# A written-out instruction order for a graph network, replaced by another from the same search

## The chip, the cores and the metric

The kernel runs on one core of one Trainium2 chip. The time is device microseconds of one execution; the kernel before took 2856.57 us as the median of three runs (2853.59 to 2860.73). One execution was also recorded by the hardware profiler: that is the profile below. The line numbers (L1916) are those of the kernel before; every line of the kernel after ORDER stands three lines lower once the change is made.

## The reference

A batch of 32 node sets x (512 nodes, 256 features each) passes through four layers over one 512 x 512 adjacency matrix. After each layer the layer's input is added to its output and the sum is normalised over its features.

```python
# layer 0: 8 heads of 32; scores = q k^T / sqrt(32), masked by adj, softmax, times v; norm;
#          relu(x w1 + b1) w2 + b2; norm
# layer 1: one additive head; e = leaky_relu(s1[i] + s2[j]), masked, softmax, times h
# layer 2: e = leaky_relu((x W1)(x W2)^T), masked, softmax, times (x W3), relu
# layer 3: 4 additive heads of 64, masked, softmax, times q, elu
x = _layernorm(x + _L0_gnn_ref(x, adj, ...), axis=-1)
x = _layernorm(x + _L1_gnn_ref(x, L1_gnn_W, L1_gnn_a, adj), axis=-1)
x = _layernorm(x + _L2_gnn_ref(x, adj, L2_gnn_W1, L2_gnn_W2, L2_gnn_W3), axis=-1)
x = _layernorm(x + _L3_gnn_ref(x, adj, L3_gnn_W, L3_gnn_a), axis=-1)
```

All of it is float32.

## The kernel before, in words

Each of the 32 node sets is a graph of about 340 steps. A step is one call of `plan(engine, ns, run, reads, writes, ...)`: an engine, a planned duration, the function that issues its instructions, and the buffers that it reads and writes. All graphs have the same steps, and some seven of them are under way at any time. `prepare` (L1624) adds the steps that load and rearrange weights and masks.

**What sets the order.** For each of the five engines (PE, DVE, ACT, POOL, SP), ORDER holds one long string. A letter names the graph (`.` is `prepare`, `A` is graph 0, `f` is graph 31), and digits ahead of a letter say how many of that graph's waiting steps on this engine are skipped. So the strings are the queues of the engines, written out. They came from a search that was done beforehand and is not in the file. Within an engine the queue is in order: a step that waits holds up every step behind it.

`Plan.follow` (L1411) reads the strings and then replays the queues with the planned durations. From that replay come three things only: which of its kind's buffers a step gets (the one that comes free first in the replay), the order in which the instructions are emitted, and nothing that delays an instruction on the chip. `Plan.ways` (L1395) picks for each projection or product whether it runs as whole 128 x 128 matmuls or as four 128 x 32 column tiles, so that PE changes its array mode less often.

PE works in three modes, and each change between neighbouring steps costs time: whole array (transposes L1784, L1867, L1899, L2059 and most of L1595), row tiles (`exps`, L1916: the scores of four heads at once, 32 rows each) and column tiles (the heads' products L1974 and L2180, the sums L1947 and L2156, and the rest of L1595).

**The steps that the text speaks of.** In layer 0, `exps` makes scores in four PSUM banks, ACT exponentiates them into a `p` buffer (L1920, four instructions), DVE multiplies the whole buffer by the mask (L1967), and PE multiplies by v (L1974). The sums over heads are made by adding `p` buffers to one another with accumulating DMAs that POOL issues (`add_dma`, L1854), and one more DMA from SP; a `p` buffer is free only when these have landed. There are eight `p` buffers. The last graph makes its sums on PE instead (`at_once`).

In layers 1 and 3, `gates` (L2044) transposes a few scores on PE (L2059), sends them to DRAM and back spread over all partitions (two DMAs from SP), and DVE builds the attention from them (L2086, L2165), masks it (L2089, L2172), and PE uses it (L1595, L2180). `add` (L1842) is an addition or product on POOL; `normalise` is L1825 and L1826 on DVE, L1829 and L1830 on ACT, L1832 on DVE, L1835 on ACT.

`load` in `prepare` (L1625) issues one weight or mask DMA from SP. In the plan each is a step of 450 ns. Graph inputs x are loaded from SP as well (L2218, 512 KB each), results stored (L2224). After the last step a short check of ranges runs on DVE and PE (L2243 to L2251).

```python
for e, steps in order.items():
    queues[e], at = [], 0
    for step in steps:
        if step.isdigit():
            at = 10 * at + int(step)
        else:
            queues[e].append(left[e, GRAPHS.index(step) - 1].pop(at))
            at = 0
```

The file holds `Plan`, `fast_path` and what is in it twice; the later copy (from L1325) is the one that runs.

Of the kernel before, what the change touches and what calls it, by code (L numbers as in the profile page):

```python
# [32 lines left out]
        "AA2.2...A2A1.2A.AA.1...A2.A1..1A1BB2AA2AA1BABAA1B1AB2ABA2ABABA1BCA2BC3BC4BB3C2C4BBBCCBCB1B2BBCDABABA"  # L33
        "D1CACDDDAADAA1CAAD2C3CDCCB2CEBCABBA2AA1AA2CEA3CCCBBCBBDB1AAAAECB1D1AEAD1AA1A1AAABAAB1DBDB1A1AAACBDCB"
        "CDCEB1AEAE1A2A1AAD1CCDAC1BBB1DB2DCDEC2DDDBBCBBDB1B1B1BBBAEFB2B1BB1CC1ACCACDCA1EDBBDDCE1E1B1BB2EFBFFB"
        "3EEAEEDC1CACAA1EDCDD2EFE2EDDCCEE2C1CECCCCCCB1FFC1CCC1DDFFE1B1D1DDBECDB1FEEDCGG1CCC2FFFC1G1FFGB1FBDD"
        "1EEC1BBF1F1DDEE2F3FEFGFCF1DDE3DDDDDDDDGFGD2DDDGEEG1E1ECFECDFEFFC1GDHEHD2D2G1HD3GDGCGHGFD2E1GGCECCEF"
        "1G1FFEG1GFF2GGDEEGEGEH2E2E3E2E1EEHH1EEE1FFE1F1FFHDGDHGFGGED1HEF1II3EEE2HEIH2HHIDH1HGFDEF1DDGFG2HFGH"
        "2HHGH1HFGIFEHHFFFFFFFFIIF1FFFGGI2G2GGGEHEHIHFHE1IF1JJGF1FF2IJIFI1IIEHJEGFIIEHGGE1IGHIH1II1IJ1HHGGFII"
        "2GGGGGGGGJJG1GGG1HHJHIHHFFJIHGIIF1JG1KKH1GG2J3JGGJJKFJIKGFH1JJFHFH1JIH2JIIJJ1JIIGJJ1HHKHH1H1HHHHH1KK"  # L40
        "1HH1HHIIGK1IIIGJKJIJHJG1KH1LLIH1H2KKHL2KHKKGJHLJGI1KGK1I1KGIJIJ2K3KJKJKHIIKK1IILI1I1I1I1ILIL1I1IIIJJ"
        "L2JJJHKHLKJ1KKIH1LIJMM2III2LMILL1LML1LIHJLHKKHHJ1LJ2LJ1KK3LLKLIKL1JJMLJJ1J1J1J1J1JJ1MM1J1JJJMKKI2K1K"
        "LKIMLK1LJLJI1M1NKN1JJ2MMN1JJ2MLMINM1MJKIMIKILK1MLLK2M3MM1LMLJM1KKNMKK1K1K2K1K1K1NKNK2K1KKLLNJLJM1LNM"
        "1LLMMJ1KK1N1OKL1KOK2NNOO2NJKNNJMKL1NNJLM1NJ1MLML2NNO2NMMLLNKNNLLL1L2L1LLL1OO2L1LLLMMO1MK1MNKON1MM1NN"
        "LK1OL1PMPL2LL2OPOO1OKLONKPNLK1OMK1N2O2MMMN1OO1ONO1ONLO1MMP3M1MMMMMMOM1PPM2MMM1NNLN1NPNLOPONOOML1PM1Q"
        "QNMM2P1MMQ3PLPQP2PLOMN1LLPNP1PONONO2PPO2PPMONNQ1NNPPN1N1NNNNQQNNNNOOQOOOMMPQPOPNNPM1QR3NONR2Q1NQQN1Q"
        "RNR2QMOQQMO1PMMO1QPOP2QP3QRQPQNQPOOQOOO1O1O1O1OORRO2OOOR1PPN2PPPQNQRQPOQN1ROPSS1O1O2RRORSO1RNQSNQOR"
        "1RPRNPN1R2RPPQQRR1RSQPQPRROPPP1P1PPPPSS1PP1PP1QSQR1OQ1QQOSRQRRPO1STPQT2PP2S1PSPS1SO1TTROPSQSSOQO1SRQ"
        "1RQR2SSR2STSQRQSPS1QQQ1Q1Q1Q1QQTT1Q1QQQ1RRTRTPS1RRPSRSSQQP1TU1QRQU2T1QQUT2TTTPSQU1TPR2TTS1PRR1SPSR2T"
        "ST2TRSQTTTRURRR1RRRRRUU1R2R1RRSSQ1SUSTQSUTSTRRQ1UT2RS2URVV1RR3UUVUQUVTRSQUUQQ1S1UTS1TTS2UUU1U1TTRUSS"  # L50
        "VSSUS3S1S1S1SS1VV1SSSVTSTVRUTRTU1TTU1SUSWR1VWTS2VS1SSV2VWRVUWRST1R2VVV1VRU1TUUTT2V3VWVUUVS1TTVVTT1T"
        "1TTTTTWW2TTTTUUW2UUUSVSVW1VVUTS1WT1XXU3T1TT2WWWT1WVXTWSX1WUW1WSU1SSVUUVV2WVVU3WWTWWUX1UUUUUUUUXWX1U"
        "1U1UUVXV1T1V1VWTWVXWVU1XTUWVYY1U2XX2UXUU1XYYWUTXTV1XXTT1VVW1XVWW2XXW2XWXUXX1VVYVV1VVVVVVYYVVV1WWVY1W"
        "2WWXWUXYUV1XXU1YVZZVW2VV2YVYY1YZU1XVZXUY1YWYU1WU1YW1X2YYXWXYX1YV1WZWYWYWW1W1W1W1WWZZ2W2W1WW1XXZ1XZXY"
        "VVYXX1YY1WWV1Za1WXWaW2Za3ZZWZ2ZVZYaXVWX1VYVZXX1ZYY2ZZZ1Z1YYWZ1XaXZ2X1XXXXXXXaa2XX1XYXYa1YYYWWZaZYZXZ"
        "W1aXY1bb1X1XX2aXabZ2aWaaWbXY1aaWZW1Y1aYY1ZZ2a3aZZabXaaYYa1YYY1Y1Y1Y1YYbbY1YYYZZbZZXZaXbYaZ1aaX1bZYcc"
        "YY2bcb1YYb1bXbacXYZZ1XaX1bZ2bZ1aa3b1bab2babYbZZc1ZZZ1Zb1ZZZZ1cc1ZZZZaacaaYbYcbaabbYZdZa1cd3Z1ZZ2cZcc"
        "d1cYc1cbdZacYaYY1cbabab2c3c1bccbZaac1acdaa1a1a1aaadda1aaad1bbZbZc1bdbcb1cacaZ1de1abeaa2ddad1deZd1dZa"
        "ebcc1bZZbb2ddc2d3dcedcca1bbddbdbbbbbbbee1b1bbb1cecda2cedadcccbda1ebfcf1bb2ee1bb2eefea1efbca1d1adcacc"
        "2ee1dd2e3eede1fe1ccdfc2ccc1cecccbfc1ccc1ddffbdd1fdefbed1ceceb3fd1ff2ff3c2c1cc4ff1ffbf1f2f3ffedcbe3fb"  # L60
        "e1ddff2f2ffffbffdeeedddd1ffdffdffdddcdeeff3f1f1ffdfdddc3e2eeece1fffcddf1d2d1deedeedcfcf1cceeeeeeeeee"
        "1ff1eeee1ff1fffefedeeeefefff1ddffd2fffffe1ed1edeffffd1ffedeee1fffff"
    ),
    "DVE": (
        ".1...6..5.3.8.1.9.7..1.4.4.1.1.3.3.5.5.1.4.1.1.2.4.4.4.4.1.3.3.3.1.2.2.2.2.2.AA.A1.A....AAAABB1BBBBB"
        "BA2ACAAAAAAACA1A1AAAAACA1A1AA2AAAACABCB1B2BBB1BBCBC3AA1AAAC1AB4AA2B2AA1A1BAAADB1BBBBBB1BBBBBDBAAAAAA"
        "AAD1A1AAA1A1A1A1AC2C1ACAC1C1C1CCCDBB1BBBD1B1B3BB1BBBBDDB2AC1C1A1CAA1A1ADCCCACA2ACC2CC1CCBCBBCBBBBBAC"
        "2A1A1AAA3BB1BBA1B1B1B1BA1AAA1BEBD2DDD1DDEDEDC1CCECDCC1CAEC3CAA2CC5B1CCBAECEBBB2ADE2D1DADB5BA1DD1ABD"
        "1BA2BDCCCDCC3DCCCDDD1DDBA2BD1BC1BB1BC1BC2CCB3C2CB1CB1CEFEE1E3EF1E1E1EF2DE2D1DDDCFDBDB3D2DBF1DDFDCDC"
        "1CCDCFFEB2E1E2BE1EBEBEBCBEEEEE2D2DDDDDDD1C1E1EEE1CCBCD2D2CD1CCDC1D2D4C1D1DDC2CD1CCCFF1FFF2FFGFGFGEEE"  # L70
        "EEGCCE1E2ECGE1EG2DDDE1EEDEDFG2FGC1F2CFFFCDFD2CD1CFFC10DFEEEF1EEEEFE2FFFDFD1EDDCE1DED1DE1E1E1E1EDDD1E"
        "DGE1G4GG1GHG1GGHH1FGFFFFHFD1D3FDFF1FH1FFH1EEFEEFEGHDH2D1DDGG1GDGGDEGGGG1GGFEFFFEFDFFF2G1GGE2EGEEFE2E"
        "F2E1FFEFEF2FEFFEEFH2HH2H1HH1HIHIHI1GGGGGIEEG3GG2GGIE1GIG1FGFFFGIFIHH3H1H1HHEHFF1F1EE2HHHHE1EGEGGHGGE"
        "GGG3F2H1HHFH1FGF1G3FGG2G1G4F2GFF1F1GFFGGFIII1I2I2IJIIJIJ1H1HHHHJH3HFFFHHJ1H1HJHG1GH1GGGJHJIFF2I1G2F"
        "2FGGII1II1FFI7GIIIHH1IHIHHHHH2I1IIGFIG1GG1HH1H1GH2H1H3GGG2H1H1GG1HGJ2J1JJK1J1J1JJKJHKI2IIIIKGGKI1HIG"
        "I3I1I1II1HI1HHKIHKKHG1GJ1JJ1G1JHGJ1GJGJ8HJ1HII1JIIIJIII8H1JJJJJ3HJHG2H1IHI1H1IIIIHI1IH1HIHIHKK1KKKL"
        "2KKKLKL1J2J1JJJLHHJ3JHJ2JLLJJJJ1II1IIJILLKH1K2H1K1HKHK1HKHK1IKKI2KHJIJJKJJJJ1KKJ1KK4I6IKII2I5I1JII1J"
        "JJ1JII1JJ1JJIJILLL1L1L1LM1LM1LMK1KL1KKKMKII3KK2KIMKM2JKJK3JK1JJKJMMIL2LL1IIL1LLJI1ILILKLKLLK2L1KKKKK"
        "LL1J10J4JJKL6J3JL1JJ2JJ2KIKJK2K1KJ1K1KJ1KM1MM2M1MN1M1MN1MNK3L2LLLLNLJJJKN1K1LN1KL3L1LL1LLK1KL1KKNN2M"
        "1MJ4M3M1M1M2JJJ1M1JJ1M2M1M2ML1MLLLLLMLL1MM1KKMJ4K1K7KMK2LL3KLKL1L1LK1LK1LKK1LKN2N1NN1NLNONNONOM1MMMK"  # L80
        "MKMO3MOKM1M1MM1LMOM2LLLMLOKO2KK1N2KNKK3N1N1N1LNNLNNM2NMNM1MMMKNMM1N1NN1LLNL2L2LLLMMLMM2M3LLL1M2M1MMM"
        "LLOO1OOO2OOOPOPP1N1NNNNLPNL3NLPNNP2NN3MNN2M1MMNMPPO2O1OO8M1OL1MOMOLLLLLOOO1ON1NNONLNNNN2O1OO1MMNOM1M"
        "M5M1N3MN2MMN2NM3N1N1NM1NMPPP4P2PQQ2P1PPPQ3O1O1OOOQO3OM1MM1N1OOQ1OO1N1OOQO2N1NNNQPQM2PP1MP1PP1MMP1MMP"
        "5NPP1N1PONO1POP1OO1OOO1PPN4NNPMON1N3NNOOON2O3O2NO1OONNONQ2QQQR2QQQQRQP2P1PPRPRNP3PNPNR2PRP1PPO1OP1OO"
        "PORRNQ1NQO3QQQQN2NQ1NNQQ10O2QPOQPPQPPPPPO1Q1QQ9OO6O2OQONP1OOO1PPPOP1PPOPOPPRRRS2R3R2R1RS1RSQ1QQQQSOQ"
        "OQO3QS2QRQSPQP1P1QQPPQRSSO1R1RR1RR8PO2O2ORPRROORQ1QQ1QQQQRQ2PO3RRP1RRP5PR1PP1QP2PPQ1P1Q3QQP1Q2Q1QPQP"
        "QSSS1S3S2S1STT1ST1R2RRRRTSR3RPT1PTPRR2R2QRRR2QQRQQTTSSPS2S2P1SQSP2PQS1P5QPSRSSR1SSRRR1QRRR2QSS8Q7QSP"
        "2QQSQ2QQ1RRQRR1R1RQ1R1RQ1RTTR2TTU1TU2T1TU1T2S2SSSSUSQ1QQ3SU1STSRRR1SUSSSR1RSRUUT2T1TQTTT2QQTQRQTQ1T"
        "1TTSS2SST1S1SSSTR1TT3R3RR4RTRRQ1S1SRSRS4S3S2R1SR1SR1SRUUU3U2UV1U1UVV1T1U2TTTTRVU1RTVS3TR1TS3TVTT1S1T"
        "SSSTVTVU1USR1UU1RSUUR2RURURUTT2UUTUTTTTT1URSUU2SS1SU2TSTT4S4SST2TS3T2TS1TSS1TSVVV2V1V2V1VW1VWVW3U1U"  # L90
        "1UUUWUSW1S3UUS2UU1UU2TU3TW1T1TU1TW1VV2V1VW1VVSV2S1TTS2SVSVVSVUUUUUTUUU2VS2V5TVV3T3T1T2T1UVTTT2U1UU1U"
        "2T2U2U1U2TU1TUTTW2WW1WX1WWXWW2VWX1VVVVXTV1T3VTXV2VV1VXUV2UVUUUXV1TXWTU1W3T1TWWW1TT5UWWWWWTVVWVVVVVV"
        "8U1U1UW1WWWUWUUVU2UVVV2V3U2VU1VU1VU1VXU1XX2X1X1XY1XYXXY2WWWWWYUWU6VVU3WY1WWY2V1VV2WWWWVVWYX1XY1UU1X"
        "2V1UXXVX2UXUUXXWXW1XVW1WWXWWUWX4V1X3VXX2VV2W2W5V1W3VWV1V1W1W1VV2W1WWWVY1YY1Y1YYZ1YYZYZ2X2X1XXXZXV1VX"
        "2X2XVX1XXZZX2W2WWWW1YXZZY1YYYY1V3VYVWVWV2YYY1YVW4WXXXYXXXXX2YYYYWW2WWVXWWX1X2WX1X3X1X1X2W1X1WWWZZZ2Z"
# [479 lines left out]
PE, DVE, ACT, POOL, SP, DMA = "PE", "DVE", "ACT", "POOL", "SP", "DMA"  # L575
# [177 lines left out]
def fast_path(  # L753
# [82 lines left out]
    plan = Plan({kind: len(tiles) for kind, tiles in buffers.items()})  # L836
# [483 lines left out]
PE, DVE, ACT, POOL, SP, DMA = "PE", "DVE", "ACT", "POOL", "SP", "DMA"  # L1320
# [972 lines left out]
```

## Time and profile before

| | |
|---|---|
| median of three runs | 2856.57 us |
| the profiled execution | 2854.66 us |
| its span, first to last instruction | 2852.9 us |
| mean granted clock of TensorE | 0.992 |
| matmuls recorded on PE | 19322 |
| DVE, ACT, POOL busy | 81%, 65%, 33% of the span |
| DMA from POOL (`p` into `p`) | 325 MB, 58.2% of the 16 engines' span |
| DMA from SP | 96.75 MB, 11.2% |
| `p` DMAs of 1 MB, issue to landing | 7.6 us (median) |
| first matmul starts | 8.57 us |
| last step of the plan on PE starts | 2833.4 us |

A line of the profile names the source line, the engine, the operation and its buffers (out<-in), with counts. "Idle before" is the time for which the engine had nothing running ahead of that instruction, and an arrow names what ended it. Matmuls of one step overlap, so two steps are compared by the starts of their first matmuls.

### The profile page before, as it was taken

What the parts mean: (1) busy time and instruction counts of PE and PEld (TensorE: products, weight loads), DVE (VectorE), ACT (ScalarE), POOL (GpSimd) and SP (SyncE); (2) the same over time, 40 slices, a digit from 0 to 9 for tenths busy, and PEclk for the clock granted to TensorE, in tenths of its full rate; (3) what the DMA queues carried; (4) which work ended last, traced back from release to release, by engine and by line L of the source; (5) the groups of instructions that cost most, each with busy time, mean ns of one, the idle gap of its engine ahead of it and who ended that gap; (6) DMA issues with size and microseconds to landing.
All of it is one profiled execution on the core that took longest, in us unless ns stands there. A gap on an engine that the chain in (4) does not pass through costs nothing.

```text
span 2852.9 us, 50322 instructions
## 1 busy us (share of the span) xinstructions
PE 2780.6 (97%) x19322; PEld 1516.4 (53%) x19322; DVE 2314.9 (81%) x4076; ACT 1858.9 (65%) x4104; POOL 939.4 (33%) x962
## 2 busy tenths in 40 slices
PE   8999999999999999999999999999999999999996
PEld 3355555555545555555555555555455555554562
DVE  5577878788888787888888888888887888888877
ACT  5566667676666666667666666666666666676553
POOL 0233333323333333333332343333343233333212
PEclk9999999999999999999999999999999999999998
DMA  6766777777777777777777777767677776775125
GB/s 176 155 130 137 157 170 152 155 164 156 156 161 158 156 159 154 152 154 159 159 157 150 158 161 152 165 145 164 145 156 155 159 163 137 172 154 118 38 62 129
DMA packets 76615, 425.12 MB, mean 149 GB/s; under 512 B 10256, under 2 KB 13456, under 8 KB 34576
## 3 DMA queue, kind: packets, MB, share of 16 engines
q0 software_dynamic: 49600, 325.08, 58.2%
q1 hardware_dynamic: 26768, 96.75, 11.2%
q8 instruction: 154, 2.52, 0.3%
q14 instruction: 93, 0.76, 0.1%
HBM read 63.38 MB, written 17.10 MB: 28 GB/s over the span
## 4 chain that ended last, share of the span: by engine, by line
PE 84%; DVE 8%; DMA 3%; ACT 3%; issue 2%; POOL 0%; SPq 0%; ACTq 0%; DVEq 0%; POOLq 0%
PE bank L1595 53%; PE bank L1916 8%; PE bank L2180 7%; PE bank L1974 6%; PE bank L1784 5%; DVE p L1967 3%; PE bank L1899 2%; DMA p<-p 1%; DVE p L2165 1%; PE bank L2156 1%; PE bank L1947 1%; PE bank L1867 1%; DMA p<-row 1%; ACT p L1920 1%; DVE st L1825 1%
## 5 line engine op out<-in xcount | busy, mean ns | idle before, releaser
L1854 POOL DMA_DIRECT2D p<-p x372 | 327.9, 902 | 1462.0 <-DMA p<-p 549.9
L1967 DVE TENSOR_TENSOR p<-p,edge_t 128x2048 f32<-128x2048 f32 x256 | 618.3, 2420 | 89.3 <-ACT p L1920 88.8
L1920 ACT ACTIVATE p<-bank 128x512 f32<-128x512 f32 x1024 | 563.9, 599 | 150.7 <-PE bank L1916 129.6
L1772 ACT ACTIVATE t<-bank 128x512 f32<-128x512 f32 x640 | 371.3, 596 | 283.8 <-PE bank L1595 115.9
L1595 PE MATMUL bank<-v,p 128*128 128x257 f32 (+1 forms) x2792 | 468.4, 381 | 3.1 <-DVE p L2089 3.1
L1595 PEld LDWEIGHTS bank<-v,p 128*128 128x128 f32 (+1 forms) x2792 | 368.0, 161 | 94.4 <-issue 25.8
L1842 POOL TENSOR_TENSOR y<-y,x 128x512 f32<-128x512 f32 x192 | 289.2, 1513 | 347.9 <-ACT y L2140 209.7
L1825 DVE BATCH_NORM_STATS2 st<-y 128x6 f32<-128x256 f32 x768 | 315.3, 411 | 81.1 <-POOL y L1842 76.4
L1835 ACT ACTIVATE x<-y,rs,rs 128x256 f32<-128x256 f32 x512 | 281.9, 594 | 52.6 <-DVE rs L1832 49.3
L1916 PE MATMUL bank<-t,t 32*128 32x512 f32 x2048 | 298.6, 637 | 1.2 <-ACT p L1920 0.7
L2165 DVE TENSOR_SCALAR p<-p,e,e 128x512 f32<-128x512 f32 x512 | 290.1, 597 | 5.8 <-DMA p<-row 4.4
L2172 DVE TENSOR_TENSOR p<-p,edge_t 128x2048 f32<-128x2048 f32 x128 | 294.0, 2299 | 1.0
L1974 PE MATMUL bank<-p,v 128*32 128x512 f32 x2048 | 263.8, 598 | 5.6 <-DVE p L1967 5.5
L2180 PE MATMUL bank<-p,v 128*32 128x512 f32 x2048 | 248.1, 597 | 8.9 <-DVE p L2172 6.3
L1595 PE MATMUL bank<-t,wqkv 128*32 128x512 f32 (+1 forms) x1088 | 247.1, 609 | 7.7 <-DMA wqkv<-in_L_gnn_w_qkv_dram 5.0
L1595 PE MATMUL bank<-t,t 128*128 128x512 f32 (+1 forms) x656 | 228.1, 593 | 1.6 <-ACT t L1772 1.6
L1772 ACT ACTIVATE v<-bank 128x512 f32<-128x512 f32 (+2 forms) x384 | 169.4, 456 | 90.5 <-PE bank L1595 89.7
L1916 PEld LDWEIGHTS bank<-t,t 32*128 32x128 f32 x2048 | 87.6, 183 | 151.9 <-issue 66.6
L1784 PE MATMUL bank<-ident,x 128*128 128x128 f32 x1024 | 146.3, 280 | 15.3 <-DMA x<-in_x_dram 8.6
L1826 DVE BATCH_NORM_AGGREGATE mv<-st 128x2 f32<-128x6 f32 x768 | 139.7, 182 | 26.2
L1784 PEld LDWEIGHTS bank<-ident,x 128*128 128x128 f32 x1024 | 116.9, 142 | 82.4 <-issue 27.7
L1835 ACT ACTIVATE y<-y,rs,rs 128x256 f32<-128x256 f32 x256 | 143.5, 596 | 17.0 <-DVE rs L1832 16.6
(119 smaller groups left out, 3835.6 us busy)
## 6 DMA issues: line engine op xcount, KB each, us to landing
p<-p POOLq DMA_DIRECT2D x248, 1024.0 KB, 7.6
p<-p POOLq DMA_DIRECT2D x124, 512.0 KB, 5.6
p<-row SPq DMA_DIRECT2D x32, 1024.0 KB
x<-in_x_dram SPq DMA_DIRECT2D x32, 512.0 KB
out_dram<-x SPq DMA_DIRECT2D x32, 512.0 KB
p<-p SPq DMA_DIRECT2D x31, 512.0 KB
e<-row SPq DMA_DIRECT2D x32, 256.0 KB
t<-in_adj_dram SPq DMA_DIRECT2D x4, 256.0 KB
```

What stands on the lines that cost most here:

```text
L1595: nc.tensor.matmul(out[c:c + w, :], left[:, c:c + w], right, start=start, stop=stop)
L1772: act(55 + n * 0.83, lambda: nc.scalar.activation(to(T(dst)), frm(T(src)), AF.Copy), [src], writes)
L1784: nc.tensor.transpose(T(bank)[:, (2 * k + c) * P:(2 * k + c + 1) * P], T(src)[:, c0 + c, k * P:(k + 1) * P], ident)
L1825: nc.vector.bn_stats(T(st)[:, c, :], T(y)[:, c, :])
L1835: act(492, lambda c=c: nc.scalar.activation(T(dst)[:, c, :], T(y)[:, c, :], AF.Identity, bias=T(nm)[:, c:c + 1], scale=T(rs)[:, c:c + 1]), ...
L1854: nc.gpsimd.dma_start(a, b, accum_op=ALU.add)
L1916: nc.tensor.matmul(T(banks[j]), T(kT)[r, g, m * P:(m + 1) * P], T(qT)[r, g, :], start=True, stop=True)
L1920: act(482, lambda j=j: nc.scalar.activation(T(p)[:, j, :], T(banks[j]), AF.Exp, scale=1.0 / math.sqrt(D0)), [banks[j]], [(p, j)])
L1967: dve(2205, lambda p=p, m=m: nc.vector.tensor_tensor(T(p), T(p), T(edge_t)[:, m, :].unsqueeze(1).to_broadcast([P, J, N]), ALU.mult), [p, ( ...
L1974: nc.tensor.matmul(T(av)[j * D0:(j + 1) * D0, :], T(v)[:, m, h * D0:(h + 1) * D0], T(p)[:, j, :], start=(m == 0), stop=(m == NC - 1))
L2165: nc.vector.tensor_scalar(T(p)[:, 2 * m + i, :], T(G)[:, h, :], T(e1)[:, r:r + 1], T(e02)[:, r:r + 1], ALU.mult, ALU.max)
L2180: nc.tensor.matmul(T(av)[w:w + 32, :], T(q)[:, m0 + m, 2 * H3 + k * P + w:2 * H3 + k * P + w + 32], T(p)[:, 2 * m + w // D3, :], start=(m0 ...
```

## The change

All five strings of ORDER are replaced, and the planned duration of a first load goes from 450 to 660 ns (in both copies of `load`). No step is added or taken away: 2391 steps on PE, 3087 on DVE, 3911 on ACT, 884 on POOL and 245 on SP, before and after. According to its short description, the new order was searched on from the one before it, with durations and landings varied a fifth more in that search. The search itself is not part of the kernel.

```diff
 ORDER = {
     "PE": (
-        "AA2.2...A2A1.2A.AA.1...A2.A1..1A1BB2AA2AA1BABAA1B1AB2ABA2ABABA1BCA2BC3BC4BB3C2C4BBBCCBCB1B2BBCDABABA"
+        "AA3.2.1..2AA1.AA1A2...A1..2.A..1A1BB2AA2AA1BAB1A1B2AB3ABAA2AABABAC1BC2B3BC4B2CB2CBB2BCBCC2B3BBDBCABA"
...
-        "1ff1eeee1ff1fffefedeeeefefff1ddffd2fffffe1ed1edeffffd1ffedeee1fffff"
+        "2fffffe1edeed1ffdff1ffedeee1fffff"
     ),
...
     "SP": (
-        "3.3.2.1.A11.11.9.9.4.12.9.2.7.1..6..4.B3.DC1.1..FEABAACBBAADCCBBEAGDDCCFBHEEDDGCIFFEEDHJGGFFIEKHHGGJ"
+        "4.14.2.2.11.A1.15.5.4.8.1.1.5.5.7..5.4.EB..C1.D.ABAACFBBAADCCBBAEGDDCCFBHEEDDGCIFFEEDHJGGFFEIKHHGGJF"
...
@@ load, in both copies
-            plan(SP, 450, run, [], [dst], lag=lag)
+            plan(SP, 660, run, [], [dst], lag=lag)
```

In the built programs the steps move by little. On PE 1319 of 2391 steps stand at another place in the queue, half of all by at most one place and none by more than 10. On DVE 2273 steps move (median one place, at most 30), on ACT 3174 (two places, at most 30), on POOL 587 (one place, at most 16), on SP 42 (at most 17, all but a few of them among the first loads). The mode of a step follows from the order: 868 instead of 817 of the 1088 projections and products run on the whole array, and neighbouring PE steps differ in mode 697 times instead of 714.

## The prediction

> **What bounds the kernel now.** I read the page first, for the engine that is full.
>
> ```profile
> PE 2780.6 (97%) x19322; PEld 1516.4 (53%) x19322; DVE 2314.9 (81%) x4076; ACT 1858.9 (65%) x4104; POOL 939.4 (33%) x962
> ```
>
> PE is full. An order can gain there in two ways alone: fewer changes of the array's mode, and less standing still. Where it stands still is told by the busy time by stretches (PE, PEld, DVE, ACT, POOL, granted clock, DMA share, GB/s):
>
> ```profile
> 0.00:100.00 100.00, 82.84 (x596) 35.71 (x596) 48.53 (x84) 48.87 (x97) 11.01 (x25) 0.93 0.76 181
> 100.00:200.00 100.00, 95.05 (x721) 48.10 (x721) 70.87 (x119) 66.78 (x142) 32.15 (x33) 0.98 0.68 136
> 200.00:2500.00 2300.00, 2286.72 (x15987) 1252.91 (x15980) 1913.66 (x3339) 1540.19 (x3410) 796.50 (x804) 1.00 0.74 156
> 2500.00:2835.00 335.00, 315.84 (x2026) 179.54 (x2024) 273.57 (x510) 193.61 (x436) 96.94 (x98) 0.99 0.45 101
> 2835.00:2853.00 18.00, 0.19 (x2) 0.09 (x2) 8.26 (x28) 9.48 (x22) 2.79 (x2) 0.51 0.25 92
> ```
>
> In the long middle PE is idle for 13.3 of 2300 us. The ends of matmuls are modelled and overlap, so I also took the starts of all 2391 PE steps and subtracted the usual pitch of each kind. That gives a budget of the execution: 8.6 us to the first matmul, 2745.8 us of steps and mode changes, 79.5 us of stalls (18.8 before 100 us, 9.3 to 200, 21.6 in the middle, 29.4 to 2833), and 19.5 us from the last plan step on PE to the end: 2853.4, against a span of 2852.9. Outside the span lie 1.8 us, so the execution took 2854.66, 1.9 under the median of the three runs.
>
> The stalls have names in the table of waits on PE, and in the chain of waits between 60 and 90 us:
>
> ```profile
> PE bank L1784 <- DMA x<-in_x_dram: 8.6, 1, 8.6
> PE bank L1784 <- ACT x L1835: 6.4, 9, 1.7
> PE bank L2180 <- DVE p L2172: 6.3, 6, 2.1
> ...
> PE bank L1974 <- DVE p L1967: 5.5, 8, 1.8
> PE bank L1595 <- DMA wqkv<-in_L_gnn_w_qkv_dram: 5.0, 1, 5.0
> ```
> ```profile
> 64.95 11.15 DMA p<-p
> ...
> 76.63 8.26 DMA p<-p
> ```
>
> The start waits for x and then for wqkv. Between 65 and 100 us all eight `p` buffers hang on accumulating DMAs that land after 11.15 and 8.26 us while the DMA engines are full (share 0.97 and 1.03). In the middle it is DVE that is late now and then.
>
> **The mode changes.** Their price is read from the starts in the timeline of PE:
>
> ```profile
> 564.50 1.88 PE L1595 MATMUL bank<-t,w_sb 128*128 128x512 f32 x4
> 566.31 1.14 PE L1916 MATMUL bank<-t,t 32*128 32x512 f32 x8
> 567.38 1.94 PE L1595 MATMUL bank<-v,p 128*32 128x257 f32 x32
> 569.14 1.90 PE L1595 MATMUL bank<-t,w_sb 128*32 128x512 f32 x16
> 570.85 1.04 PE L1974 MATMUL bank<-p,v 128*32 128x512 f32 x8
> 571.82 1.14 PE L1916 MATMUL bank<-t,t 32*128 32x512 f32 x8
> ```
>
> The same product takes 1.81 us ahead of a row-tile step (564.50 to 566.31), against a usual 1.717: leaving the whole array costs 93 ns. In column tiles it takes 1.71 to its next neighbour (569.14 to 570.85): the tiling itself costs nothing. The medians over all steps: leaving the whole array 93 ns, row tiles 109, column tiles 114; entering row tiles 101, column tiles 25, the whole array 56 (transposes) to 104. Counted in the built orders, the changes go from 714 to 697: whole to row +5, row to column -7, column to row -12, whole to column -4, column to whole +1, row to whole 0. So 5 x 194 - 7 x 134 - 12 x 215 - 4 x 118 + 194 = -2.8 us, all of it on the full engine.
>
> The Trainium skill says in "TensorEngine Tiling (Array Packing)", under Key Properties, that a change of the tiling mode drains TensorE. By the rule alone one would price each of 17 changes at an emptied array: by the trace's largest pair (215 ns) -3.7 us, were all of that kind. The trace prices each pair and includes a +5 that costs, so I keep -2.8. The 51 steps that go back from column tiles to the whole array cost nothing either way (1.717 in both).
>
> **The first loads.** The 660 in place of 450 delays nothing on the chip: it enters the replay, and with it the choice of buffers. The loads are issued by SP already about 0.67 us apart (32 DMAs from 0.76 to 21.5 us). What moves is their order. wqkv is the 17th DMA instead of the 16th, one issue later (0.67 us), and a weight of 256 KB more lies ahead of it, 0.9 us at the 274 to 281 GB/s moved there. Either the issue or the bytes set it, or in part both: +0.7 to +1.6, I take +1.0, since PE starts on wqkv at 18.37 directly after its landing. x of graph 0 moves from fifth to sixth; its PE steps end 5 us ahead of wqkv, so up to 5 us are hidden, and past that it costs in full. Graph 4's x is now loaded ahead of graph 1's, whose transposes start at 37.8 us, some 16 us after all loads have been issued: hidden.
>
> **The stalls to 200 us.** POOL's first 13 additions of `p` are issued in the same order, and PE asks for the same eight buffers within a step or two. Between a graph's scores on PE and its first waiting product, the path through two DMAs (2.9 us of stall at 164.0) has the same 11.5 us of PE work over it as before. I take 0, with -4 to +4: below nothing, because a stall that stays short also spares the lower clock (0.83 between 80 and 100 us).
>
> **The middle.** Here one looks at how much PE work lies between the scores (L1916) and the product (L1974) of one buffer, priced as above. Of 264 such pairs 95 have under 10 us before and 75 after; under 8 us 34 and 27. The median goes from 11.3 to 12.0. For layer 3, from the transpose to the first L2180, the median goes from 23.95 to 24.25. So the tight pairs are a fifth fewer. If the 21.6 us of stalls follow them, -4.3; if nothing follows, 0; if the stalls vanish, -21.6. I take -4. ACT, DVE, POOL and SP steps moved past one another cost nothing themselves while PE has work: that cover is the median 12 us, and where it is gone, the lateness comes through in full.
>
> **The tail.** A transpose pair of graph 31 (idle 1.22 and 0.44 at 2791 us) moves behind one more 1.74 us product. That fills the gap, but from 2790 to 2830 DVE is busy for 37.8 of 40 us, and only its own wait of 0.71 us can shrink. Earlier, near 2687, one 1.74 us step fills part of 3 us. I take -1.5, between 0 and -4. The check at the end does not change.
>
> Sum: -2.8 + 1.0 + 0 - 4 - 1.5 = -7.3 us. 2854.7 becomes 2847.4 for the profiled execution, and the median 2856.6 becomes 2849.
>
> **The rivals.** *Slower by DVE and POOL blocking each other.* Two rows of the timeline, POOL and DVE:
>
> ```profile
> 2032.52 3.42 POOL L1842 TENSOR_TENSOR y<-y,bb_row 128x512 f32<-128x512 f32 x1
> ```
> ```profile
> 2034.72 6.22 DVE L2165 TENSOR_SCALAR p<-p,e,e 128x512 f32<-128x512 f32 x3
> ```
>
> Three instructions of 0.54 us take 6.22 beside POOL's work, and PE stands 2.6 us at 2046. "SBUF — State Buffer", section Who interferes with whom, has the rule: the two engines take a shared port exclusively, for a whole instruction, and which is blocked depends on who issued first. It speaks against any reshuffling: 2273 DVE and 587 POOL steps have new neighbours, and a plan cannot hold a meeting to the nanosecond. By the rule each meeting could cost up to 3.8 us (L2165's longest is 4.34); by the row DVE as a whole lost 34 us on L1967 (256 x (2.420 - 2.288)), yet all of PE's stalls in the middle are 21.6. The point is the cover: a hold counts once it exceeds what the pair has left. If four more such holds reach PE, at 3.8 us, that is +15: 2856.6 - 2.8 + 1 + 15 = 2870. Against it stand the longer covers.
>
> *The stalls go.* If spread landings keep PE fed, the middle loses 14 of 21.6, the early stretch 4, the tail 4: 2856.6 - 2.8 + 1 - 22 = 2833. For it: the planned landing of a 1 MB addition is 6.3 us, the measured one 4.5 to 13.9, so margin for landings is what was missing. Against it: the tight pairs fell only by a fifth, and POOL's holds are not landings.
>
> *Nothing is left of it.* The start costs 1.6, stalls are redrawn to the same sum, the tail stays bound by DVE: 2856.6 - 2.8 + 1.6 = 2855. The change then does not do what it says.
>
> **How the numbers follow.** Forecast 2849 (own range 2843 to 2855) 0.45; stalls go 0.2; nothing left 0.17; slower 0.18. A measurement can tell about 0.3%, or 8.6 us: below 2848, above 2865. Faster: 0.21 of the forecast, 0.2 of the second, 0.41. Slower: 0.16 of the blocking, 0.03 of odd ends of the others, 0.19. The rest, 0.40, is the same. The range takes in most of both outer cases: 2834 to 2867.
>
> **What would show it.** 697 mode changes at the old prices; the first wqkv matmul at 19 to 20 us; stalls of about 17 us between 200 and 2500; an unchanged stretch from 65 to 100 us; the last PE steps 7 us earlier. I am wrong if the idle time in the middle grows past 13 us, with L1967 or L2165 longer in the mean than 2420 and 597 ns, or if the early stretch moves by over 4 us.

## The result and the profile after

The kernel after takes 2843.37 us as the median of seven runs (2841.34 to 2847.61); the kernel before, measured beside it, takes 2853.59 (2850.74 to 2860.73, also seven). The ratio is 0.9963, with a 95% interval of 0.9952 to 0.9975: 10 us faster. The forecast was 2849, or 7.3 us less than before; taken from the 2853.59, that is 2846, at the slow end of the interval. The range that it gave holds the time. Its working holds much less well than its sum.

The page of after, the line of the engines:

```profile
PE 2774.5 (98%) x18554; PEld 1527.8 (54%) x18554; DVE 2320.7 (82%) x4076; ACT 1854.2 (65%) x4104; POOL 962.4 (34%) x962
```

The busy time by stretches, in the columns of the prediction (the last three: granted clock, DMA share, GB/s):

```profile
0.00:100.00 100.00, 82.51 (x612) 36.12 (x616) 50.04 (x84) 50.62 (x100) 10.95 (x25) 0.95 0.75 176
100.00:200.00 100.00, 97.89 (x845) 48.35 (x845) 70.05 (x123) 67.40 (x143) 34.48 (x36) 1.00 0.77 153
200.00:2500.00 2300.00, 2279.96 (x15117) 1263.73 (x15110) 1923.89 (x3335) 1535.21 (x3406) 814.31 (x801) 1.00 0.73 155
```

The last of these is the surprise: PE is idle for 20.0 of 2300 us, where it was 13.3. The table of waits on PE, over the whole execution, gives the names:

```profile
PE bank L1787 <- DMA x<-in_x_dram: 10.1, 1, 10.1
PE bank L1787 <- ACT x L1838: 7.0, 8, 2.1
...
PE bank L1598 <- DMA wqkv<-in_L_gnn_w_qkv_dram: 4.1, 1, 4.1
PE bank L1977 <- DVE p L1970: 3.6, 9, 1.0
...
PE bank L2183 <- DVE rs L1835: 2.9, 1, 2.9
PE bank L1950 <- DMA p<-p: 2.6, 1, 2.6
```

Between 200 and 2500 us alone, the same table adds up to 9.2 us before and 10.3 us after that DVE ended, 3.3 and 6.1 us that ACT ended, and 0.2 and 2.8 us that a DMA ended. So DVE still ends most of PE's waiting there, at other places than before; the increase lies with ACT and with one DMA. (A held DVE instruction can stand behind ACT: ahead of the wait at 574 us two L2168 take 2.73 us.) In the chain of waits between 60 and 90 us, one of the two DMAs is left:

```profile
76.08 9.23 DMA p<-p
```

The budget of the prediction (first PE step, steps and mode changes at their usual price, stalls by stage, what follows the last PE step), made for every traced execution but that of `b_660`:

| kernel | first | steps and modes | stalls to 100 | to 200 | to 2500 | to 2650 | later | end | span |
|---|---|---|---|---|---|---|---|---|---|
| before | 8.6 | 2745.8 | 18.8 | 9.3 | 22.0 | 3.5 | 25.8 | 19.5 | 2852.9 |
| after | 10.1 | 2743.2 | 15.5 | 4.3 | 30.6 | 0.5 | 21.7 | 17.0 | 2842.4 |
| after again | 10.2 | 2743.2 | 15.2 | 4.3 | 28.5 | 0.5 | 22.4 | 16.8 | 2840.6 |
| early | 10.8 | 2745.8 | 16.8 | 4.2 | 19.6 | 4.5 | 26.0 | 19.6 | 2846.9 |
| middle | 9.9 | 2743.7 | 18.0 | 9.3 | 27.9 | 2.6 | 26.5 | 18.7 | 2856.1 |
| tail | 9.2 | 2745.3 | 18.3 | 9.3 | 19.9 | 0.5 | 28.6 | 18.8 | 2849.4 |
| both ends | 10.3 | 2745.3 | 17.7 | 5.7 | 19.2 | 1.5 | 21.6 | 18.5 | 2839.5 |
| early and middle | 10.5 | 2743.7 | 16.4 | 4.2 | 29.1 | 2.6 | 25.9 | 19.0 | 2851.0 |
| wqkv sooner | 11.2 | 2743.2 | 12.2 | 4.2 | 30.7 | 0.5 | 21.7 | 17.0 | 2840.4 |
| tail, code moved | 8.1 | 2745.3 | 17.6 | 10.3 | 32.8 | -0.1 | 29.7 | 19.8 | 2863.1 |
| both ends, code moved | 11.3 | 2745.3 | 16.7 | 8.8 | 23.2 | -0.1 | 29.8 | 18.0 | 2852.5 |
| after, small additions | 10.4 | 2743.2 | 15.9 | 3.7 | 5.8 | 1.5 | 20.6 | 17.2 | 2817.9 |
| before, small additions | 8.3 | 2745.8 | 18.4 | 4.7 | 5.5 | 3.2 | 23.0 | 18.8 | 2827.3 |

From before to after: +1.5 first step, -2.6 modes, -3.3 and -5.0 early, +8.6 in the middle, -3.0 and -4.1 in the tail, -2.5 at the end. "Steps and modes" is worked out from the order and the usual prices; whatever makes a step longer than usual falls under the stalls.

**What a stall costs besides.** One thing makes steps longer: the granted clock of TensorE. Its records in the trace come in pieces of 3.4 us. In before it is 0.50 for 6.8 us from 84.4 us, for 3.4 us from 132.1 and from 2047.0, and for 6.8 us from 2688.7, each time on a stall of PE or directly behind it; not every stall is followed by such a piece (those of 1.5 and 1.3 us at 1007 and 1011 us are not). Two products of 1.72 us each take 6.4 us at 85.6 us. The stretch from 80 to 100 us, before and then after:

```profile
80.00:100.00 20.00, 16.37 (x120) 4.68 (x116) 7.20 (x4) 8.11 (x17) 2.61 (x3) 0.83 1.03 201
```
```profile
80.00:100.00 20.00, 16.67 (x144) 5.29 (x140) 10.10 (x5) 9.98 (x20) 2.61 (x3) 0.91 1.00 197
```

Up to the end of the plan the pieces at 0.50 add up to 27 us in before, 20 in after (14 in its second trace), 17 with both ends, 37 in the tail alone, 37 with both ends and code moved, and 48 in the tail with code moved. Where PE is full, half of such a piece is lost.

### The profile page after: what moved, and what is told of

Its sections match the earlier page's. It is cut to its first block, busy times and chain, and to the rows that moved or that the text cites. A ratio compares the mean times of both kernels' runs of the same rounds, so it can differ in the third digit from the quotient of the medians.

```text
span 2842.4 us, 48818 instructions
## 1 busy us (share of the span) xinstructions
PE 2774.5 (98%) x18554; PEld 1527.8 (54%) x18554; DVE 2320.7 (82%) x4076; ACT 1854.2 (65%) x4104; POOL 962.4 (34%) x962
## 3 DMA queue, kind: packets, MB, share of 16 engines
q1 hardware_dynamic: 26768, 96.75, 11.3%
## 4 chain that ended last, share of the span: by engine, by line
PE 79%; DVE 10%; ACT 4%; DMA 3%; issue 3%; POOL 1%; SPq 0%; DVEq 0%; ACTq 0%; POOLq 0%
PE bank L1598 50%; PE bank L1919 8%; PE bank L2183 6%; PE bank L1977 6%; PE bank L1787 4%; DVE p L1970 4%; DMA p<-p 3%; PE bank L1902 2%; PE bank L1950 1%; ACT p L1923 1%; DVE st L1828 1%; PE bank L1870 1%; DVE p L2168 1%; PE bank L2159 1%; ACT x L1838 1%
## 5 line engine op out<-in xcount | busy, mean ns | idle before, releaser
L1970 DVE TENSOR_TENSOR p<-p,edge_t 128x2048 f32<-128x2048 f32 x256 | 633.4, 2479 | 95.4 <-ACT p L1923 95.0
L1598 PEld LDWEIGHTS bank<-v,p 128*128 128x128 f32 (+1 forms) x2600 | 370.0, 167 | 94.8 <-issue 26.5
L1845 POOL TENSOR_TENSOR y<-y,x 128x512 f32<-128x512 f32 x192 | 284.2, 1492 | 364.0 <-ACT y L2143 205.0
L2175 DVE TENSOR_TENSOR p<-p,edge_t 128x2048 f32<-128x2048 f32 x128 | 297.3, 2326 | 0.8
L1919 PE MATMUL bank<-t,t 32*128 32x512 f32 x2048 | 292.7, 636 | 0.0
L2168 DVE TENSOR_SCALAR p<-p,e,e 128x512 f32<-128x512 f32 x512 | 284.9, 586 | 1.7 <-ACT p L1923 1.0
L1775 ACT ACTIVATE v<-bank 128x258 f32<-128x258 f32 (+2 forms) x384 | 169.5, 458 | 70.1 <-PE bank L1598 67.4
L1787 PE MATMUL bank<-ident,x 128*128 128x128 f32 x1024 | 146.3, 278 | 18.0 <-DMA x<-in_x_dram 10.1
L1598 PEld LDWEIGHTS bank<-t,t 128*128 128x128 f32 (+1 forms) x596 | 95.0, 175 | 111.0 <-issue 100.7
```

What stands on the lines that cost most here:

```text
L1598: nc.tensor.matmul(out[c:c + w, :], left[:, c:c + w], right, start=start, stop=stop)
L1775: act(55 + n * 0.83, lambda: nc.scalar.activation(to(T(dst)), frm(T(src)), AF.Copy), [src], writes)
L1787: nc.tensor.transpose(T(bank)[:, (2 * k + c) * P:(2 * k + c + 1) * P], T(src)[:, c0 + c, k * P:(k + 1) * P], ident)
L1919: nc.tensor.matmul(T(banks[j]), T(kT)[r, g, m * P:(m + 1) * P], T(qT)[r, g, :], start=True, stop=True)
L1970: dve(2205, lambda p=p, m=m: nc.vector.tensor_tensor(T(p), T(p), T(edge_t)[:, m, :].unsqueeze(1).to_broadcast([P, J, N]), ALU.mult), [p, ( ...
L2168: nc.vector.tensor_scalar(T(p)[:, 2 * m + i, :], T(G)[:, h, :], T(e1)[:, r:r + 1], T(e02)[:, r:r + 1], ALU.mult, ALU.max)
```

## The experiments

**The constant, and one stage of the order at a time.** The stage of a step is where the replay of before's plan starts it: up to 200 us, up to 2500, and behind. All these kernels have the 660 ns. First the constant alone (`b_660`), then one stage each in after's order. Of the strings, the first change in PE's is shown, cut out of its row:

```diff
 b_660, load
-            plan(SP, 450, run, [], [dst], lag=lag)
+            plan(SP, 660, run, [], [dst], lag=lag)
 h_early, up to 200 us
-        "AA2.2...A2A1.2A.AA.1...A2.A1..1A1BB2AA2AA1BABAA1B1AB2ABA2ABABA
+        "AA3.2.1..2AA1.AA1A2...A1..2.A..1A1BB2AA2AA1BAB1A1B2AB3ABAA2AAB
 h_mid, 200 to 2500 us
-        CEB1AEAE1A2A1AAD1CCDAC1BBB1DB2DCDEC2DDDBBCBBDB1B1B1BBBAEFB2B1BB1CC1ACC
+        CEB1AEAE1A1AAA1CDCDCA1BBB1DB2DCDEC2DDDBBCBBB1B1BBDBBAEF2BB1BBCC1ACAD2C
 h_tail, behind 2500 us
-        ebfcf1bb2ee1bb2eefea1efbca1d1adcacc2ee1dd2e3eede1fe1ccdfc2ccc1cecccbfc
+        ebfcf1bb2e1be2eebfae1eafc1d1aab1ccd2eec1dd2e3e1feddee1ccf2cccc1cccecbf
```

> The order of before, with the planned duration of a first load at 660 ns instead of 450: only the choice of buffers in the replay changes. Theory A (what the two traces show: the new order gains at both ends of the run and loses in the middle): the constant itself is worth nothing, 0 us within 3. Theory B (the gain before 200 us comes from the better planned start, through the buffers): 6 to 8 us faster than before, and the stalls before 200 us fall from 28 to about 20 us.

> The steps that the plan starts in its first 200 us stand in the order of after, all others in the order of before (714 mode changes, as before; loads at 660). Theory A: the first matmul 1.5 us later, 8.3 us fewer stalls before 200 us, the rest as before: 7 us faster than before. Theory B (each reordering redraws the stalls of the whole run): the early gain may be there, but the sum is unrelated to it, between 8 us faster and 8 us slower. Theory C (what is gained early is waited for again at the DMA-bound sums of p or in the tail): within 2 us of before.

> Only the steps that the plan starts between 200 and 2500 us stand in the order of after (700 mode changes instead of 714, so -2.2 us of work on PE; loads at 660). Theory A: the middle's stalls rise from 21.6 to about 31 us as in the trace of after: 5 to 8 us slower than before. The step of my prediction (stalls in the middle fall by 4): 6 us faster than before.

> Only the steps that the plan starts after 2500 us stand in the order of after (711 mode changes; loads at 660). Theory A: stalls from 2500 us on fall by 7.2 us and the end behind the last step on PE by 2.5: about 10 us faster than before. The step of my prediction (the tail is bound by DVE and can win 1.5 us): 2 us faster. Theory C (the tail's gain in the trace was given by what arrived ahead of it, not by its own order): within 2 us of before.

| | us | ratio to before | 95% interval |
|---|---|---|---|
| b_660 | 2854.86 | 1.0004 | 0.9995 to 1.0013 |
| h_early | 2848.68 | 0.9982 | 0.9973 to 0.9991 |
| h_mid | 2862.82 | 1.0028 | 1.0019 to 1.0038 |
| h_tail | 2851.21 | 0.9996 | 0.9987 to 1.0005 |

The constant is worth nothing that can be measured. The early order gains 5 us (7 expected), the middle loses 8 as theory A had it, and the tail alone moves by -1, inside its interval, where theory A expected -10. Together that is +2, and the whole gives -10: the stages do not add.

**Two stages at a time.** `h_ends` joins the rows of `h_early` and `h_tail`, `h_earlymid` those of `h_early` and `h_mid`; middle and tail without the early order were not run:

```diff
 PE, up to 200 us (both)
-        "AA2.2...A2A1.2A.AA.1...A2.A1..1A1BB2AA2AA1BABAA1B1AB2ABA2ABABA
+        "AA3.2.1..2AA1.AA1A2...A1..2.A..1A1BB2AA2AA1BAB1A1B2AB3ABAA2AAB
```

> The order of after for what the plan starts in its first 200 us and after 2500 us, that of before in between. Theory A (the gain lies at both ends, the middle loses, stages add): 5.1 + 1.1 us off, about 2848, stalls between 100 and 200 us at 4, those of the middle at 20 to 22. Theory C (a stage's gain depends on what the other stages hand to it, since the three stages alone gave -5.1, +8 and -1.1 us where the whole gives -10.2): the tail gains its full share only behind an earlier queue, so 2844 or less, with the last accumulation of graph 30 landing before VectorE asks for it. Rival: the tail stays as it was alone, 2849 or more.

> The order of after up to 2500 us of the plan, that of before behind it. Theory A: -5.1 + 8, about 2856, slower than before. Theory C: what the middle lost alone came from its seam with before's first 200 us, so without the seam it loses little: 2848 to 2850, and the rest of the gain of after is the tail's behind its own middle.

With both ends in after's order and the middle in before's: 2839.03 us, ratio 0.9953 (0.9939 to 0.9966), as theory C had it. It is the lowest median of all whole kernels here, 4 us below after's, but the two intervals overlap. With early and middle: 2853.24, 1.0005 (0.9996 to 1.0014), between what theories A and C expected. By the ratios, then, the middle costs 8 us alone, 7 behind the early order, and 3 between both ends. The tail is worth 1 us alone, 8 behind the early order and 12 behind early and middle. It is the tail that does not add.

**The start, and a second trace.** In `a_wqkv` one DMA issue moves ahead of ten other first loads; `a_again` is after unchanged.

```diff
 a_wqkv, SP
-        "4.14.2.2.11.A1.15.5.4.8.1.1.5.5.7..5.4.EB..C1.D.ABAACFBBAADCCBBAEGDDCCFBH
+        "4.14.2.2.11.A..14.4.3.7...4.4.6.5.4.EB..C1.D.ABAACFBBAADCCBBAEGDDCCFBHEED
```

> After, with the load of wqkv moved on SyncE's queue to directly behind x of graph 0 (one move, nothing else). If the start is bound by that load, the first wqkv matmul comes about 3 us earlier and TensorE's first stall shrinks by as much. Theory: the end gains 2 to 3 us only if the stretch from 65 to 100 us, which waits on the accumulating DMAs, takes it over; the rival is that the stall at 76 us (p of an early graph landing) grows by what the start gains, so that the time is within 1 us of after, and the sum of stalls to 100 us stays at 15 to 16.

> After, unchanged, for a second trace: how far the stalls of one stage differ between two executions of one program. If the stalls are set by the order, each stage within 3 us of the first trace (15.5, 4.3, 30.6, 0.5 and 21.7 us); if they hang on how transfers happen to collide, the middle and the tail differ by 5 us or more, and single stages can't be told apart by one trace.

`a_wqkv` took 2843.19, ratio 0.9971 (0.9961 to 0.9981). In its trace PE is 2.8 us ahead, and the gain passes through the DMA-bound stretch unharmed: the landing of 9.23 us starts at 73.26 in place of 76.08. Of this nothing shows in the measured time. Against the second trace of after, 1.0 us is lost again ahead of the first step and 2.2 in the middle. The theory held for the stretch, not for the end. The second trace of after has the stages within 2.1 us of the first, most of them within 0.7, and of the 11 stalls over 0.9 us that either has in the middle, 10 are over 0.75 us in both. So the places of the stalls belong to the program, and are not drawn anew in each execution; their lengths can change (2.6 and 1.3 us for the DMA at 959 us).

**The tail: where TensorE's code is fetched.** In `h_tail`, the chain of waits has three DMAs that it lacks in after:

```profile
2774.38 3.59 DMA row<-gT
2778.10 6.54 DMA p<-row
...
2798.59 6.95 DMA p<-row
```

and the table of waits on DVE between 2765 and 2835 us begins with a row that the same table of `h_ends` and of after lacks:

```profile
DVE p L2165 <- DMA p<-row: 6.6, 2, 4.4
```

This is the round trip of graph 30's and 31's scores through DRAM. By the records of landings, the first half of graph 30's trip (`row<-gT`) takes 1.52 to 1.56 us and the second (`p<-row`) 4.5 to 5.4 in eleven of the fourteen traces of this study. The DMA table of `h_tail` for 2774 to 2778.2 us holds one packet of another queue:

```profile
q8 instruction: 1, 0.02, 1.4%
```

It is a fetch of 16 KB of code, started at 2775.94 (there are 154 on this queue in the execution, 2.5 MB beside PE's 39,000 instructions, so I take them for PE's); the engine that served it carried one of the 16 parts of `row<-gT`, and that part came 2.1 us behind the other fifteen: its packet began at 2776.87, when the fetch ended. A second fetch at 2799.7 lies on graph 31's trip. After has 148 of these packets beside its 37,000 instructions on PE, which fits the same reading. To move the fetches without moving any step, 50 small matmuls go ahead of PE's first instruction:

```diff
             def run(bank=bank, c0=c0):
+                for _ in range(0 if shifted else 50):
+                    nc.tensor.matmul(T(bank)[:16, 0:1], ident[:, :16], ident[:, 0:1], start=True, stop=True)
+                shifted.append(1)
```

> The kernel that has the order of after behind 2500 us alone, with 50 small matmuls (16 columns of weights, 1 column of data, on the identity matrix, into the bank that the first transposes then overwrite) put ahead of TensorE's first instruction, where it waits for x anyway. Nothing else changes in any queue but TensorE's place in its code: 100 instructions, where one fetch of code (16 KB, the queue called instruction) covers some 256 and comes every 24 us there, so the fetches move about 9 us forward. Theory D (the tail's gain was lost there because a fetch at 2775.9 and one at 2799.7 us fell on the two round trips of graph 30's and 31's rows: one of the 16 engines brought row<-gT after 3.59 us where 1.5 is usual, and p<-row after 6.5 and 6.95 where 4.5 is usual): the fetches fall at about 2767 and 2790, VectorE's waits for p<-row (6.6 us) go, and the time falls by 4 to 7 us, to 2844 to 2847. Rival (the tail's gain needs the earlier stages in after's order for another reason): 2850 to 2852, as without the small matmuls.

> The same 50 small matmuls ahead of the kernel with after's order at both ends and before's in the middle. There the fetches at 2764.5, 2784.9 and 2808.6 us miss the round trips (2771.2 to 2777.3 and 2789.0 to 2794.9); 9 us earlier the second comes at about 2776, on p<-row of graph 30. Theory D: that landing takes 1 to 2.5 us longer, and the time grows by 1 to 5 us, to 2840 to 2844, so that the same edit moves the two kernels in opposite directions. Rival (the small matmuls do something of their own, such as a warmer clock at the start): both kernels move the same way.

| | us | ratio to before | fetch after `row<-gT` of graph 30 is issued | that DMA | `p<-row` |
|---|---|---|---|---|---|
| h_tail | 2851.21 | 0.9996 | 1.6 us | 3.59 | 6.54 |
| h_tail_n | 2855.63 | 1.0008 (0.9999 to 1.0018) | 1.2 us | 3.43 | 6.09 |
| h_ends | 2839.03 | 0.9953 | none within the trip | 1.52 | 4.46 |
| h_ends_n | 2854.44 | 1.0005 (0.9996 to 1.0014) | 1.6 us | 3.65 | 6.39 |

The expectation for `h_tail_n` failed: the fetch fell on the same DMA once more. The reckoning of where the fetches go was wrong (each small matmul shows as two matmuls in the trace, so the shift was some 200 instructions and not 100, and the fetches do not move by the count alone). `h_ends_n` went the way expected, and by 15 us instead of 1 to 5. By its trace 8 us of that are in the stalls behind 2650 us, 3 between 100 and 200 us and 4 in the middle. Both kernels moved the same way, as the rival had it, but the rival's reason (a warmer clock) would have made them faster, and the mean granted clock was lower: 0.991 in the traced execution of `h_ends_n` where `h_ends` has 0.995. The two traces differ by 13.0 us; PE's idle time differs by 3.4 of that, and the pieces at a clock of 0.50 by 20 us, which is up to 10 us of lost work. In `h_tail_n` the tail stayed as it was. Its ratio is 0.0012 above that of `h_tail`, and the two intervals overlap, so its slowing is not clear of noise. The traced execution shows 13 us more stalls in the middle, but it lies 9 us above its median: seven executions of this kernel took 2851.5 to 2857.4 us and four 2861.8 to 2864.9.

So it is shown that in the three traces with a fetch on the first half of graph 30's trip that half was late by about 2 us, and the second by 1 to 2, and in none of the eleven without; graph 31's second half, too, took 7.0, 7.6 and 7.5 us in these three, with a fetch on it. DVE waits 6.6, 6.9 and 7.0 us for `p<-row` there, the clock falls to 0.50 twice behind 2780 us, for 6.8 us each (once for 3.4 in after), and the stalls behind 2650 us are 28.6 to 29.8 where after, its second trace and `h_ends` have no such wait and 21.6 to 22.4 (`b_pool`, with its small additions, has 6.0 us of it and only 23.0). The stretch of `h_tail` and of after:

```profile
2750.00:2800.00 50.00, 46.34 (x235) 29.20 (x238) 35.60 (x64) 24.08 (x57) 9.61 (x11) 0.93 0.45 98
```
```profile
2750.00:2800.00 50.00, 47.89 (x269) 28.88 (x268) 37.78 (x69) 24.83 (x60) 9.84 (x11) 1.00 0.47 119
```

It is shown as well that small matmuls at the start, with the order unchanged, cost 15 us in one kernel. That the fetch is what made the tail depend on the other stages is the likeliest reading: those change how far PE's code has got by then. It was not shown by a kernel that loses its fetch and gains the time, and a fetch is not the only cause: no fetch lies on the second half of graph 30's trip, and in `b_pool` graph 31's trip took 3.11 and 6.47 us with none on it.

**The middle: DVE held by POOL.** In `a_pool` and `b_pool`, after and before, five of POOL's six kinds of in-place additions work on 2 of 256 columns and leave the others out.

```diff
+        n = C if op == ALU.mult else 2
-            T(dst)[:, w, :], T(a)[:, w, :],
-            T(b)[:, w, :] if row is None else T(row).unsqueeze(1).to_broadcast([P, 2, C]), op),
+            T(dst)[:, w, :n], T(a)[:, w, :n],
+            T(b)[:, w, :n] if row is None else T(row)[:, :n].unsqueeze(1).to_broadcast([P, 2, n]), op),
```

> After, with five of GpSimd's six kinds of in-place additions cut to the first 2 of 256 columns of each tile (the additions in the other columns are left out; the multiplication stays whole), so that GpSimd occupies memory for a small part of its 1270 ns per instruction. Theory E (the middle of the new order loses because VectorE's instructions are held up by GpSimd's at more places that TensorE waits on: holds beyond an instruction's median length sum to 89 us in after and 76 us in before): the holds fall below 30 us, and the middle's stalls from 30.6 us to 12 or less. Rival (the middle's stalls are in the order of VectorE's own queue and in the accumulating DMAs): they stay above 20 us.

> Before, with the same additions cut. Theory E: its middle stalls fall from 22 to about the same number as those of after with this cut (difference under 3 us where it was 9), since the difference was holds; the whole then differs by 2.6 us of mode changes, 8 us of stalls before 200 us and 7 to 10 us at the end, more than the 10 us of the whole kernels. Rival: the difference of the middle stays at 5 us or more.

2819.73 us for after (ratio to before 0.9875, 0.9860 to 0.9890) and 2830.85 for before (0.9918, 0.9903 to 0.9933). The stretch from 200 to 2500 us, first `a_pool`, then `b_pool`:

```profile
200.00:2500.00 2300.00, 2295.42 (x15291) 1278.63 (x15284) 1843.66 (x3378) 1550.29 (x3445) 523.68 (x809) 1.00 0.74 157
```
```profile
200.00:2500.00 2300.00, 2298.04 (x16037) 1263.88 (x16030) 1845.51 (x3371) 1552.44 (x3441) 505.33 (x808) 1.00 0.74 157
```

PE's idle time of 20.0 and 13.3 us becomes 4.6 and 2.0. The stalls of the budget go to 5.8 and 5.5, and their difference from 8.6 to 0.3. By idle time the difference goes from 6.7 to 2.6, and most of what is left is the one wait for a DMA that after has at 959 us and `a_pool` still has:

```profile
PE bank L1952 <- DMA p<-p: 2.0, 1, 2.0
```

So this wait is not shown to come from the holds. What DVE's instructions take beyond the median of their kind in this stretch (excesses over 0.1 us, all kinds) falls from 121 and 105 us to 18 and 20; the 89 and 76 of the expectation do not come out of this count, but their difference does, nearly. Practically all of it lies on instructions beside which an addition or product ran on POOL. It goes with the middle's order: 102 to 109 us in the traces with before's middle, 117 to 122 in those with after's. Theory E held for the holds and for the stalls of the middle. Its sum did not: it had the two kernels 18 to 21 us apart with the cut, and they are 11, because the early and late stalls of before shrink as well. One thing is not told apart: the smaller additions also end sooner (in the commonest kind 482 ns in the mean against 1492 in after), and whatever waited for one got it earlier.

## Why the prediction was right and wrong

**Mode changes (-2.8): right.** 697 of them, at the old prices (the whole-array product takes 1.81 us ahead of a row-tile step in after too); the budget has -2.6.

**First loads (+1.0): about right.** The first wqkv matmul starts at 18.9 us instead of 18.4, a little under the +0.7 to +1.6 given, and the stall ahead of it is 0.9 us shorter since x came 1.5 later. The constant is nothing, as said.

**Stalls to 200 us (0, from -4 to +4): wrong, -8.3.** The failed step is "the path through two DMAs (2.9 us of stall at 164.0) has the same 11.5 us of PE work over it as before". It counted PE's cover, which is indeed the same (12.2 and 12.8 us from the transpose of the scores to the product's turn), and not what happens on the path. The chain of waits of before there:

```profile
155.94 5.62 DVE p L2086 x4
...
161.58 2.30 DVE p L2089
...
164.01 7.99 PE bank L1595 x134
```

Four instructions of 0.54 us take 5.62. The line's own statistics (min, median, max) in this window, before and then after:

```profile
L2086 DVE TENSOR_SCALAR p<-e,e,e x4: 534/535/4240, 155.9 to 161.0; 128x512 f32<-128x512 f32 x4
```
```profile
L2089 DVE TENSOR_SCALAR p<-e,e,e x4: 529/548/675, 151.6 to 153.2; 128x512 f32<-128x512 f32 x4
```

One was held for 3.7 us, and in after none is: from the transpose to the end of the mask product the path takes 14.9 us and then 11.5, and the stall of 2.9 us is gone. POOL in before, beside the hold:

```profile
155.81 1.58 POOL L1842 TENSOR_TENSOR y<-y,bb_row 128x512 f32<-128x512 f32 x1
157.03 0.41 POOL L2082 MEMSET v<- 128x4 f32 x1
157.09 2.80 POOL L1842 TENSOR_TENSOR x<-x,be_row 128x512 f32<-128x512 f32 x2
```

With POOL's additions cut, before loses its stalls here too (9.3 to 4.7), after hardly (4.3 to 3.7). The rest of the gain is in good part the clock: the piece at 0.50 from 132 us is gone and that from 84 us is half as long, up to 3.4 us of the 8.3. The prediction had named the lower clock as the reason for its range, and its range was too narrow.

**The middle (-4): wrong in sign, +8.6.** The failed step is that the stalls would follow the number of tight pairs, which fell by a fifth. The covers did grow, and the holds grew as well. (The 21.6 us of stalls that it starts from are 22.0 in the budget; with 21.6 its parts add up to 79.1 and not to its 79.5.) The groups of the mask product in 200 to 2500 us (busy, mean ns, idle before), before and then after:

```profile
L1967 DVE TENSOR_TENSOR p<-p,edge_t 128x2048 f32<-128x2048 f32 x214 | 519.4, 2432 | 44.6 <-ACT p L1920 44.3
```
```profile
L1970 DVE TENSOR_TENSOR p<-p,edge_t 128x2048 f32<-128x2048 f32 x213 | 528.8, 2488 | 52.5 <-ACT p L1923 52.2
```

With medians of 2284 and 2291 ns, its holds go from 32 to 42 us, and those of all of DVE from 105 to 121. Idle time in the middle and a longer L1967 are what the prediction had named as the sign that it is wrong. The largest stall of after is 3.1 us at 2046 us. The timelines of POOL and DVE in after:

```profile
2036.65 1.58 POOL L1845 TENSOR_TENSOR y<-y,x 128x512 f32<-128x512 f32 x1
2037.89 1.57 POOL L1845 TENSOR_TENSOR y<-y,g_row 128x512 f32<-128x512 f32 x1
...
2042.61 1.58 POOL L1845 TENSOR_TENSOR y<-y,bb_row 128x512 f32<-128x512 f32 x1
```
```profile
2036.00 3.76 DVE L2168 TENSOR_SCALAR p<-p,e,e 128x512 f32<-128x512 f32 x2
...
2042.50 3.85 DVE L2175 TENSOR_TENSOR p<-p,edge_t 128x2048 f32<-128x2048 f32 x1
2046.27 0.15 DVE L1835 SCALAR_TENSOR_TENSOR rs<-mv,rs 128x4 f32<-128x4 f32 x1
```

Two L2168 take 3.76 us in place of 0.97, and L2175 takes 3.85 in place of 2.28; PE's next product waits for the L1835 behind them. This is the rival "slower by DVE and POOL blocking each other", at its place and at about half of its price (+8.6 where +15 was put; up to 2.6 of the 8.6 is the wait for a DMA at 959 us, whose cause stays open). It was given 0.18 as a case of its own, though it can stand beside gains elsewhere; it does, with both signs: a hold fewer also made part of the early gain. The Trainium skill ("SBUF — State Buffer", Who interferes with whom) says that the two engines take a shared port exclusively for a whole instruction; the runs agree in so far as the holds go when POOL's additions become small.

**The tail (-1.5): wrong in size, -7.1, and -2.5 behind it.** The failed step is "from 2790 to 2830 DVE is busy for 37.8 of 40 us, and only its own wait of 0.71 us can shrink". The window was cut at the wrong place: that full stretch begins with graph 30's attention, and it can begin sooner. DVE's timeline in before and in after:

```profile
2789.87 0.53 DVE L2165 TENSOR_SCALAR p<-p,e,e 128x512 f32<-128x512 f32 x1
```
```profile
2783.66 0.99 DVE L2168 TENSOR_SCALAR p<-p,e,e 128x512 f32<-128x512 f32 x2
```

It begins 6.2 us sooner, since graph 30's scores leave SP at 2775.6 in place of 2781.8, and 3.0 us of that are stalls gone between 2500 and 2650 us. In before DVE also waits 3.1 us for two landings of `p<-row`, in after not at all. Of the 2.5 us at the end, which the prediction held to be unchanged, 1.1 are one hold: L1832 takes 1.22 us at 2838.6 in before, beside an addition on POOL, and 0.13 in after. The rest of it stays open. In `h_tail` the trip is left earlier still (2774.4), and DVE begins at 2784.74: there the landing is what is late.

**The sum** of -7.3 came near -10.2 because an early gain and a tail gain that were not seen were paid for by a middle loss that was not seen either. That it fits is luck. Of the signs that the prediction set, the mode changes and the last PE steps came (2825.4 us, 8 earlier); the 17 us of stalls in the middle and the unchanged stretch from 65 to 100 us did not, and both signs of being wrong, the idle time of the middle and an early stretch that moves by over 4 us, came. "The stalls go" and "nothing is left" both failed.

## What to carry to other kernels

Where PE waits for a chain over other engines, count what can stretch the chain (a hold by another engine, a DMA that shares its engines with others) beside the PE work that covers it: here holds made both the gain at 164 us and the loss in the middle. A stage at the end that is full on one engine is still worth what its beginning can be moved. A change of an order is best split by stages, in pairs too: the lowest median here came from both ends of the new order without its middle. And a stall of PE can cost more than its length, through the clock behind it: here up to half of 6.8 us.

## What the runs showed of the hardware

Fetching TensorE's code uses the same DMA engines as data: in `h_tail` a 512-byte packet of `row<-gT` began only when the fetch on its engine had ended. The Trainium skill ("Runtime: NRT & Kernel Launch", Instruction fetch mechanics) says that a sequencer fetches its code in blocks of 16 KiB by a DMA queue of its own, and calls the cost mostly hidden. The size agrees with the packets seen here. What it costs the engine that runs the code, no run here measures; a data DMA that meets the fetch is not always spared. A fetch of 16 KB mostly takes 0.9 to 1.5 us of one of 16 engines, and half of them follow the last after 14 to 22 us (`h_tail`). On graph 30's 8 KB DMA it made 3.4 to 3.7 us of 1.5, in all three traces that have one there. Over all fourteen traces, SP issues the `p<-row` that waits for such an 8 KB DMA 1.45 us after it in the median of 345 trips with no fetch, and 2.66 us in 66 with a fetch that began from 0.3 us before to 1.4 us after its issue; eight of these 66 were not held, and other traffic is not kept apart in these figures.

And 50 small matmuls in otherwise idle time, 2.8 us in all, made one kernel 15 us slower; in the other nothing is clear of noise. So a difference between two orders can hang on something other than the order, such as the place in TensorE's code; what it was here stays open. Up to 10 of the 13 us between the two traces lie in the granted clock.
